# Two graph layers on one core: a new instruction order for the first two groups, the set-up's weight sums on three engines, and one transpose moved behind one addition

## The chip, the cores and the metric

The kernel runs on one core of a Trainium2 chip. The metric is the device time of one execution in microseconds; the median of three runs of the kernel before is 2593.3 us (2591.22 to 2593.96).

## What is computed

The input x holds 128 graphs of 128 nodes with 512 features. Two layers follow each other, each on a layer norm with ReLU, each added to its input. In the reference's terms, cut to what matters:

```python
h = maximum(layernorm(x), 0)
q, k, v = h @ Wq0.T, h @ Wk0.T, h @ Wv0.T
rel = adj.T * (q @ k.T)
x = x + (rel / norm(rel, axis=2)) @ v                       # layer 0
h = maximum(layernorm(x), 0)
q, k, v = h @ Wq1 + bq, h @ Wk1 + bk, h @ Wv1 + bv          # 8 heads of 64
x = x + softmax(q @ k.T / 8 + mask(adj == 0)) @ v           # layer 1
```

All of it is float32.

## The kernel before, in words

The 128 graphs are worked in 32 groups of four. Five products of a 512x512 matrix with a group's turned h (512 features x 512 nodes) carry most of the arithmetic: g and v of layer 0 (g is h times Wq0.T Wk0, a matrix made once in `weights0`), and Q, K, V of layer 1. Each is a `Product`, done with seven half-sized products P1 to P7 instead of eight (the method of Strassen and Winograd). For this each weight matrix is kept as seven 256-column parts: three plain quarters and four sums T1, T2, T3, T4N, made once by `sums` (lines 91 to 96); the fourth plain quarter, `w12`, is needed only for the sums. The data side has four sums too, s0 to s3 (`sumA`, `sumB`). P1 to P7 accumulate in three PSUM banks x, y and z: P6, P7 and P4 are added on top of what P1 left in bank x, P3 on top of P5 in bank z. ScalarE or VectorE copies the bank out after P1, P5 and P6 (`keep`), and VectorE adds a kept part to the bank and writes a quarter of the result after P2, P3 and P7 (`add`, line 232). So **P7 must wait until the copy after P6 has read bank x, and P4 until P7's addition has read it.**

h has to be turned, features on partitions. In the first group TensorE does it against an identity (`turn_pe`). In all others it is done through memory: `hn` (ScalarE) writes the normalised rows, sends them to DRAM, `rd` (SyncE's queue) fetches them back in blocks, and `T` (VectorE, line 303) turns 32x32 blocks of what came back. `T0` makes the first half of h (two graphs), `T1` the second. P1 and P2 read the first half, P5, P6, P3 need sums over both halves, P7 needs another sum, P4 the second half.

Other steps that the prediction names: `stat` (VectorE, means and variances) and `inv` (GpSimd, four small operations that make scale and shift) come ahead of `hn`. `R` makes rel for four graphs, `mask_rel`, `square`, `N` and `norms` mask it and make the norms (the last step on GpSimd), `O` multiplies rel with v and `xO` adds to x. `S`, `mk`, `ex`, `wr`, `wt` are scores, mask with row maximum, exponentials with the way to DRAM, the fetch, and the turning of the softmax weights; `A` multiplies them with v; `oc`, `rdo`, `ot` turn and add the output. GpSimd adds to x and stores.

The order of work is written out by hand: the schedule is manual on all five engines, so every engine executes its instructions in the order in which they are issued, and `run` issues one step after another from a list of names. In a step's name, p is layer 1 of two groups ago, l layer 1 of the last group, m layer 0 of this group, n layer 1 of this group, f layer 0 of the next. There is one list, `ORDER` (lines 517 to 526), used for all 32 groups, and `LAST` for the tail. In the first group p and l do not exist and their steps are skipped, and so are m's steps of turning. The set-up ahead of it is `weights0`, `turn_pe` twice, `weights_v0`, and `weights1`, which scales Wq1 and bq and makes twelve sums, all on GpSimd.

Buffers that matter: four PSUM banks for the products (`ps_mm`), two for rel, O and A (`ps_o`), one pair for the scores (`ps_s`). Each half of h and each s has a single buffer per layer.

Of the kernel before, what the change touches and what calls it, by code (L numbers as in the profile page):

```python
# [9 lines left out]
F32 = mybir.dt.float32  # L10
AF = mybir.ActivationFunctionType
ALU = mybir.AluOpType
AX = mybir.AxisListType

P = 128
# [6 lines left out]
def kernel(  # L22
# [15 lines left out]
    nc = tc.nc  # L38
    B, N, D = x.shape
    assert N == P and B % G == 0  # L40
    KD = D // P
    H, HD = 8, 64
# [20 lines left out]
    ps_o = ctx.enter_context(tc.tile_pool(name="ps_o", bufs=2, space=PSUM))  # L63
# [4 lines left out]
    def load(g: int, b: int, queue):  # L68
        xb = xpool.tile([P, D], F32, tag="xb", name=f"xb_{g}_{b}")
        queue.dma_start(xb, x[g * G + b])  # L70
        x_tiles[g, b] = xb

    for b in range(G):
# [13 lines left out]
    wc = {  # L87
        n: const.tile([P, 7, 2, HF], F32, tag=f"wc_{n}", name=f"wc_{n}") for n in ("a", "v0", "q", "k", "v1")
    }

    def sums(n: str, w12, eng):
        c = wc[n]
        eng.tensor_tensor(c[:, T1], w12, c[:, W11], ALU.subtract)
        eng.tensor_tensor(c[:, T2], c[:, W22], c[:, T1], ALU.subtract)
        eng.tensor_tensor(c[:, T3], c[:, W22], w12, ALU.subtract)
        eng.tensor_tensor(c[:, T4N], c[:, W21], c[:, T2], ALU.subtract)
# [11 lines left out]
    bq_sb = const.tile([P, NH], F32, tag="bq", name="bq_sb")  # L108
    bk_sb = const.tile([P, NH], F32, tag="bk", name="bk_sb")
    bv_sb = const.tile([P, H * HD], F32, tag="bv", name="bv_sb")  # L110
    w12 = {}

    def place(n: str, m: int, ps, w12, copy):

        copy(wc[n][:, W11 if m < 2 else W21, m % 2, :], ps[:, 0:HF])
        copy(w12[:, m, :] if m < 2 else wc[n][:, W22, m % 2, :], ps[:, HF:D])

    def weights0():

        a12 = rpool.tile([P, 2, HF], F32, tag="r", name="a12")  # L120
        pa = [ps_mm.tile([P, D], F32, tag="mm", name=f"pa_{m}") for m in range(KD)]
        for k in range(KD):
            for m in range(KD):
                nc.tensor.matmul(
                    pa[m], lhsT=raw["q"][:, k, ts(m, P)], rhs=raw["k"][:, k, :],
                    start=(k == 0), stop=(k == KD - 1),
                )
        for m in range(KD):
            place("a", m, pa[m], a12, nc.vector.tensor_copy)
        sums("a", a12, nc.vector)  # L130

    def weights_v0():
        v12 = rpool.tile([P, 2, HF], F32, tag="r", name="v12")
        for m in range(KD):
            pt = ps_mm.tile([P, KD, P], F32, tag="mm", name=f"pwv_{m}")
            for k in range(KD):
                nc.tensor.transpose(pt[:, k, :], raw["v"][:, k, ts(m, P)], ident)
            place("v0", m, pt.rearrange("p k e -> p (k e)"), v12, nc.scalar.copy)
        sums("v0", v12, nc.gpsimd)
        nc.vector.tensor_scalar(mask, adj_sb, 0.0, NEG, ALU.is_equal, ALU.mult)  # L140

    def load1():
        for name, w in (("q", wq1), ("k", wk1), ("v1", wv1)):
            wr = w.rearrange("(k p) d -> p k d", p=P)
            nc.gpsimd.dma_start(
                wc[name][:, W11 : W21 + 1].rearrange("p h k d -> p (h k) d"), wr[:, :, 0:HF]
            )
            nc.gpsimd.dma_start(wc[name][:, W22], wr[:, 2:4, HF:D])
            w12[name] = wpool.tile([P, 2, HF], F32, tag="wT", name=f"w12_{name}")
            nc.gpsimd.dma_start(w12[name], wr[:, 0:2, HF:D])  # L150
        nc.gpsimd.dma_start(bq_sb, bq1.rearrange("(e p) -> p e", p=P))
        nc.gpsimd.dma_start(bk_sb, bk1.rearrange("(e p) -> p e", p=P))
        nc.gpsimd.dma_start(bv_sb, bv1.partition_broadcast(P))

    def weights1():

        SC = HD**-0.5
        nc.gpsimd.tensor_scalar(wc["q"][:, 0:3], wc["q"][:, 0:3], SC, None, ALU.mult)
        nc.gpsimd.tensor_scalar(w12["q"], w12["q"], SC, None, ALU.mult)
        nc.gpsimd.tensor_scalar(bq_sb, bq_sb, SC, None, ALU.mult)  # L160
        for n in ("q", "k", "v1"):
            sums(n, w12[n], nc.gpsimd)


    EN = mybir.EngineType
# [89 lines left out]
    class Layer:  # L255
# [49 lines left out]
                self.u.pop(i).rearrange("p t (k q) -> p t k q", q=BK),  # L305
            )

        def turn_pe(self, i):

            half = self.half_tile(i)  # L310
            hn = npool.tile([P, 2, KD, P], F32, tag="e", name=f"hn_{i}")
            for r in range(2):
                b = 2 * i + r
                nc.scalar.activation(
                    hn[:, r].rearrange("p k q -> p (k q)"), x_tiles[self.g, b], AF.Relu,
                    bias=self.shift[:, b : b + 1], scale=self.rstd[:, b : b + 1],
                )
                pt = ps_o.tile([P, KD, P], F32, tag="po", name=f"pt_{b}")
                for k in range(KD):
                    nc.tensor.transpose(pt[:, k, :], hn[:, r, k, :], ident)  # L320
                nc.scalar.copy(half[:, :, ts(r, P)], pt)
# [29 lines left out]
    class Layer0(Layer):  # L351
        n = 0
# [54 lines left out]
    class Layer1(Layer):  # L407
        n = 1
# [105 lines left out]

    ORDER = """
        l.Q.P1 p.rdo0 l.sumA l.Q.P2 m.hn0 l.sumB l.K.P1 m.rd0 m.hn1 l.K.P2 m.rd1 p.wt3 l.Q.P5
        p.ot0 l.Q.P6 l.Q.P3 p.A1 p.oc1 p.rdo1 m.T0 l.Q.P7 l.K.P5 m.T1 l.K.P6 l.Q.P4 f.load0 f.load1
# [2 lines left out]
        l.ex1 l.wr1 l.wt0 m.R m.mask_rel m.square f.stat2 f.stat3 f.inv1 m.V.P6 m.V.P3 m.N m.norms l.S2 l.mk2  # L522
        m.V.P7 l.ex2 l.wr2 l.wt1 m.O0 m.xO0 m.O1 m.xO1 n.stat0 n.stat1 n.inv0 m.V.P4 n.hn0 n.rd0 l.start_v l.V.P1
        m.O2 m.xO2 m.O3 m.xO3 n.stat2 n.stat3 n.inv1 l.S3 l.mk3 l.V.P2 l.V.P5 n.hn1 l.V.P6 l.wt2 n.rd1 l.ex3
        l.wr3 l.V.P3 n.T0 l.V.P7 l.A0 l.oc0 l.V.P4 n.T1 n.start
    """.split()
    LAST = """
        l.Q.P1 p.rdo0 l.sumA l.Q.P2 l.sumB l.K.P1 l.K.P2 p.wt3 l.Q.P5 p.ot0 l.Q.P6 l.Q.P3 p.A1 p.oc1
# [2 lines left out]
        l.V.P4 l.ex3 l.wr3 l.wt1 l.A0 l.oc0 l.rdo0 l.wt2 l.wt3 l.A1 l.oc1 l.rdo1 l.ot0 l.ot1  # L531
    """.split()

    def run(order, m=None, **who):
        who["m"] = m
        for step in order:
            name, *path = step.split(".")
            at = who.get(name)
            if at is None or (name == "m" and m.g == 0 and path[0][:-1] in ("hn", "rd", "T")):
                continue  # L540
            if len(path) == 2:
                getattr(getattr(at, path[0]), path[1])()
            elif path[0][-1].isdigit():
                getattr(at, path[0][:-1])(int(path[0][-1]))
            else:
                getattr(at, path[0])()

    with tc.manual_schedule(engines={EN.PE, EN.SP, EN.Pool, EN.DVE, EN.Activation}):
        p, l, m = None, None, Layer0(0)
        for b in range(G):  # L550
            m.stat(b)
        m.inv(0)
        m.inv(1)
        for b in range(G):
            load(1, b, nc.gpsimd)
        load1()
        weights0()
        m.turn_pe(0)
        m.turn_pe(1)
        weights_v0()  # L560
        weights1()
        for g in range(NG):
            n = Layer1(g)
            f = Layer0(g + 1) if g + 1 < NG else None
            run(ORDER, p=p, l=l, m=m, n=n, f=f)
            p, l, m = l, n, f
        run(LAST, p=p, l=l)

# [29 lines left out]
```

## Time and profile before

| what | value |
|---|---|
| median of three runs | 2593.3 us |
| the profiled execution | 2595.17 us |
| span of its instructions | 2593.4 us, mean granted TensorE clock 0.99 |
| TensorE busy | 2513.8 us (97%) |
| VectorE, ScalarE, GpSimd busy | 1701.2 us (66%), 1020.6 us (39%), 549.7 us (21%) |
| first matmul of layer 1's Q in the first group | at 80.05 us |
| the same in the second group | at 159.82 us |
| from there to the last group's | 30 groups, 77.57 to 79.63 us each |

One execution was traced. A time is the distance from the first instruction. TensorE appears twice, as PE (matmul) and PEld (weight load). Each of the seven products issues four float32 matmuls, and the trace holds two records for each of these, so that a product is a row of "x8". "DVE" is VectorE, "ACT" ScalarE, "POOL" GpSimd, "SP" SyncE. A row of the timeline gives start, duration, engine, line, operation, what is written and read, and in brackets how long the engine had been idle and what ended that.

### The profile page before, as it was taken

Reading aid. Unit: us, or ns where it says so; the run is one execution under the profiler, and the core shown is the slowest. Engines: PE = TensorE matmul, PEld = TensorE weight load, DVE = VectorE, ACT = ScalarE, POOL = GpSimd, SP = SyncE. Lnnn points to the kernel's source line nnn. Section 1 sums busy time; section 2 is a strip of 40 time slices with the busy share of each in tenths; the row PEclk is TensorE's granted clock in tenths of the full one; section 3 lists DMA queues with packets and bytes.
Section 4 is the critical chain, followed back from the end, with each engine's and each line's share of the span. In section 5 each row is a group of like instructions: output and inputs, shape, how many; then the busy total and the mean of one; then the engine's idle time right before and its main releaser. Section 6 shows DMA issues by size and latency. Waiting matters only on the chain.

```text
span 2593.4 us, 40797 instructions
## 1 busy us (share of the span) xinstructions
PE 2513.8 (97%) x14656; PEld 2135.5 (82%) x14656; DVE 1701.2 (66%) x2477; ACT 1020.6 (39%) x3245; POOL 549.7 (21%) x961
## 2 busy tenths in 40 slices
PE   8799999999999999999999999999999999999995
PEld 6688888888888888888888888888888888888884
DVE  3466766667666667666667666667666666666664
ACT  2334443344333444334444334444334344434442
POOL 6012122212122112122112221121222121222111
PEclk9899999999999999999999999999999999999997
DMA  3255444555445555445554445454445554445443
GB/s 135 98 163 194 140 147 154 175 167 183 148 137 167 171 171 180 139 145 167 167 179 158 147 143 175 160 194 149 146 145 178 163 190 144 145 156 172 162 139 130
DMA packets 374379, 409.90 MB, mean 158 GB/s; under 512 B 29920, under 2 KB 290144, under 8 KB 374176
## 3 DMA queue, kind: packets, MB, share of 16 engines
q1 hardware_dynamic: 281168, 167.92, 22.8%
q10 hardware_dynamic: 71792, 169.89, 17.6%
q0 software_dynamic: 21216, 69.49, 7.7%
q8 instruction: 115, 1.88, 0.3%
q14 instruction: 88, 0.72, 0.1%
HBM read 206.90 MB, written 200.28 MB: 157 GB/s over the span
## 4 chain that ended last, share of the span: by engine, by line
PE 80%; DVE 7%; DMA 7%; POOL 2%; issue 2%; SPq 1%; ACT 1%; DVEq 0%; POOLq 0%; ACTq 0%
PE pv_x L208 12%; PE pq_x L208 9%; PE pk_x L208 8%; PE pg_x L208 8%; PE pv_z L208 5%; PE pg_z L208 4%; PE pk_z L208 4%; PE pr L367 4%; PE pss L430 4%; PE pq_z L208 4%; DMA u_h<-d_h 4%; PE po L476 3%; PE po L399 3%; PE pv_y L208 3%; PE pq_y L208 2%; PE pk_y L208 2%
## 5 line engine op out<-in xcount | busy, mean ns | idle before, releaser
L448 ACT ACTIVATE e<-pss,nmax 128x128 f32<-128x128 f32 x1024 | 359.7, 379 | 203.5 <-DVE nmax L441 185.5
L511 POOL TENSOR_TENSOR xb<-xb,o 128x512 f32<-128x512 f32 x128 | 163.2, 1275 | 1193.4 <-DVE o L504 1191.7
L208 PE MATMUL pv_x<-wc_v,h 128*128 128x256 f32 x1280 | 301.9, 383 | 21.7 <-DVE v L232 21.3
L208 PEld LDWEIGHTS pv_x<-wc_v,h 128*128 128x128 f32 x1280 | 241.4, 191 | 74.4 <-DVE v L232 39.0
L291 ACT ACTIVATE hn<-xb,shift,rstd 128x512 f32<-128x512 f32 x252 | 190.9, 807 | 155.7 <-POOL shift L283 150.8
L208 PE MATMUL pv_z<-wc_v,s 128*128 128x256 f32 x1024 | 245.2, 382 | 0.0
L303 DVE STREAM_TRANSPOSE h<-u_h 128x1024 f32<-128x1024 f32 x126 | 156.4, 1241 | 104.3 <-DMA u_h<-d_h 103.8
L448 ACT ACTIVATION_READ_ACCUMULATOR e<-pss,nmax 128x1 f32 x1024 | 224.2, 219 | 0.0
L439 DVE TENSOR_TENSOR pss<-pss,mask 128x1024 f32<-128x1024 f32 x128 | 157.2, 1228 | 99.5 <-PE pss L430 99.3
L208 PEld LDWEIGHTS pv_z<-wc_v,s 128*128 128x128 f32 x1024 | 192.1, 190 | 28.7 <-DVE pv_r L225 0.3
L208 PE MATMUL pq_x<-h,wc_q 128*128 128x256 f32 x768 | 186.4, 386 | 14.6 <-issue 14.6
L208 PE MATMUL pv_x<-wc_v,s 128*128 128x256 f32 x768 | 184.9, 384 | 0.0
L208 PE MATMUL pk_x<-h,wc_k 128*128 128x256 f32 x768 | 181.5, 379 | 0.0
L208 PEld LDWEIGHTS pq_x<-h,wc_q 128*128 128x128 f32 x768 | 144.6, 191 | 39.0 <-issue 15.4
L273 DVE BATCH_NORM_STATS2 st<-xb 128x6 f32<-128x512 f32 x256 | 172.1, 672 | 5.2 <-DMA xb<-in_x_dram 5.2
L280 POOL TENSOR_SCALAR rstd<-mv 128x2 f32<-128x2 f32 x128 | 28.6, 224 | 648.8 <-DVE mv L274 648.6
L430 PEld LDWEIGHTS pss<-kT,qT 64*128 64x128 f32 x2048 | 124.7, 188 | 48.7 <-PE po L399 23.5
L208 PEld LDWEIGHTS pk_x<-h,wc_k 128*128 128x128 f32 x768 | 146.0, 190 | 19.8
L441 DVE TENSOR_REDUCE nmax<-pss 128x8 f32<-128x1024 f32 x128 | 156.7, 1224 | 4.4
L463 DVE STREAM_TRANSPOSE wT<-u_w 128x1024 f32<-128x1024 f32 x128 | 152.8, 1194 | 8.0 <-DMA u_w<-d_w 8.0
L208 PEld LDWEIGHTS pv_x<-wc_v,s 128*128 128x128 f32 x768 | 140.9, 190 | 20.3
L430 PE MATMUL pss<-kT,qT 64*128 64x128 f32 x2048 | 149.5, 285 | 2.5 <-ACT e L448 2.3
(134 smaller groups left out, 4438.4 us busy)
## 6 DMA issues: line engine op xcount, KB each, us to landing
d_w<-e ACTq DMA_DIRECT2D x128, 512.0 KB, 2.6
u_w<-d_w SPq DMA_DIRECT2D x512, 128.0 KB, 2.9
d_h<-hn ACTq DMA_DIRECT2D x126, 512.0 KB, 3.4
u_h<-d_h SPq DMA_DIRECT2D x504, 128.0 KB, 3.3
d_o<-oT ACTq DMA_DIRECT2D x64, 512.0 KB, 3.9
u_o<-d_o SPq DMA_DIRECT2D x256, 128.0 KB, 3.3
out_dram<-xb POOLq DMA_DIRECT2D x128, 256.0 KB, 2.8
xb<-in_x_dram POOLq DMA_DIRECT2D x124, 256.0 KB, 3.3
```

The lines of the kernel that those rows point to most:

```text
L208: nc.tensor.matmul(ps[:, m, :], lhsT=lhsT, rhs=rhs, start=first and m == 0 and k == 0, stop=k == 1, skip_group_check=True,)
L273: nc.vector.bn_stats(st, x_tiles[g, b])
L291: nc.scalar.activation(hn[:, r], x_tiles[g, b].rearrange("p (k j q) -> p j k q", j=TB, q=BK), AF.Relu, bias=self.shift[:, b : b + 1], scal ...
L303: nc.vector.transpose(half.rearrange("p k (t i) -> p t k i", i=BK), self.u.pop(i).rearrange("p t (k q) -> p t k q", q=BK),)
L367: nc.tensor.matmul(pr[:, b, :], lhsT=self.turned(k, b), rhs=self.gT[:, k, ts(b, P)], start=(k == 0), stop=(k == KD - 1),)
L399: nc.tensor.matmul(po, lhsT=self.rel[:, b, :], rhs=self.v[:, b, :], start=True, stop=True)
L430: nc.tensor.matmul(pss[:, r, k, :], lhsT=self.qT[rows, k, ts(b, P)], rhs=self.kT[rows, k, ts(b, P)], start=True, stop=True,)
L439: nc.vector.tensor_tensor(sc, sc, mask[:, None, :].to_broadcast([P, H, P]), ALU.add)
L441: nc.vector.tensor_reduce(self.nmax[b], sc, AX.X, ALU.max, negate=True)
L448: nc.scalar.activation(e[:, :, i, :], sc[:, i, :].rearrange("p (j q) -> p j q", q=BK), AF.Exp, bias=nmax[:, i : i + 1], accum_out=self.tot ...
L463: nc.vector.transpose(self.wT[b].rearrange("p h (t i) -> p t h i", i=BK), self.uw.pop(b).rearrange("p t (h q) -> p t h q", q=BK),)
L511: nc.gpsimd.tensor_tensor(xb, xb, o.rearrange("p k t q -> p (k t q)"), ALU.add)
```

## The change

Four things are done, all of them moves:

1. **Set-up.** The normalised rows of the first group's h are made by their own step `hn_pe`, ahead of `weights0`. The eight TensorE transposes of the first half are issued between the third and the fourth quarter of `weights0`'s matmuls, those of the second half behind the last quarter.
2. **Layer 1's weights.** The scaling of Wq1 and bq goes from GpSimd to ScalarE, the four sums of q and the four of k go to VectorE, those of v1 stay on GpSimd. They are no longer issued in one piece but as steps `w.scale`, `w.sumq`, `w.sumv`, `w.sumk` within the first group's list.
3. **First two groups.** They get lists of their own, `FIRST` and `SECOND`. In FIRST the second group's h is made and turned during the first group's layer 0, and the second group's seven g products (`f.G`) stand right behind the first group's O2 and O3, ahead of its layer 1. SECOND is ORDER without these steps and without the steps of p.
4. **All other groups.** In ORDER the step `n.T0` goes from before `l.V.P7` to behind it.

```diff
-    def weights0():
+    def weights0(between):
...
+            if k == KD - 2:
+                between()
...
-    def weights1():
-
-        SC = HD**-0.5
-        nc.gpsimd.tensor_scalar(wc["q"][:, 0:3], wc["q"][:, 0:3], SC, None, ALU.mult)
-        nc.gpsimd.tensor_scalar(w12["q"], w12["q"], SC, None, ALU.mult)
-        nc.gpsimd.tensor_scalar(bq_sb, bq_sb, SC, None, ALU.mult)
-        for n in ("q", "k", "v1"):
-            sums(n, w12[n], nc.gpsimd)
+    class Weights1:
+        def scale(self):
+
+            SC = HD**-0.5
+            nc.scalar.mul(wc["q"][:, 0:3], wc["q"][:, 0:3], SC)
+            nc.scalar.mul(w12["q"], w12["q"], SC)
+            nc.scalar.mul(bq_sb, bq_sb, SC)
+
+        def sumq(self):
+            sums("q", w12["q"], nc.vector)
+
+        def sumk(self):
+            sums("k", w12["k"], nc.vector)
+
+        def sumv(self):
+            sums("v1", w12["v1"], nc.gpsimd)
...
+    FIRST = """
+        m.sumA m.sumB m.start m.G.P1 w.scale m.G.P2 f.stat0 f.stat1 f.inv0 m.G.P5 f.hn0 f.rd0 m.G.P6 w.sumq
+        m.G.P3 f.stat2 f.stat3 f.inv1 m.V.P1 f.hn1 f.rd1 w.sumv m.G.P7 m.V.P2 w.sumk m.G.P4 m.V.P5
+        m.R m.mask_rel m.square f.T0 m.V.P6 m.V.P3 m.N m.norms m.V.P7 m.O0 m.xO0 m.O1 m.xO1 n.stat0 n.stat1
+        n.inv0 n.hn0 n.rd0 m.V.P4 f.T1 m.O2 m.O3 f.sumA f.start f.G.P1 m.xO2 m.xO3 n.stat2 n.stat3 n.inv1
+        n.hn1 n.rd1 f.G.P2 f.sumB f.G.P5 f.G.P6 f.G.P3 n.T0 f.G.P7 f.G.P4 n.T1 n.start
+    """.split()
+    SECOND = """
+        l.Q.P1 l.sumA l.Q.P2 l.sumB l.K.P1 l.K.P2 l.Q.P5 l.Q.P6 f.load0 f.load1 l.Q.P3 l.K.P5 l.K.P6 l.Q.P7
+        l.K.P3 l.K.P7 l.S0 l.mk0 f.load2 f.load3 l.Q.P4 l.K.P4 l.ex0 l.wr0 m.V.P1 f.stat0 f.stat1 f.inv0
+        m.V.P2 l.S1 l.mk1 m.V.P5
+        l.ex1 l.wr1 l.wt0 m.R m.mask_rel m.square f.stat2 f.stat3 f.inv1 m.V.P6 m.V.P3 m.N m.norms l.S2 l.mk2
...
     ORDER = """
...
-        l.wr3 l.V.P3 n.T0 l.V.P7 l.A0 l.oc0 l.V.P4 n.T1 n.start
+        l.wr3 l.V.P3 l.V.P7 n.T0 l.A0 l.oc0 l.V.P4 n.T1 n.start
...
         load1()
-        weights0()
-        m.turn_pe(0)
+        m.hn_pe(0)
+        m.hn_pe(1)
+        weights0(lambda: m.turn_pe(0))
         m.turn_pe(1)
         weights_v0()
-        weights1()
...
-            run(ORDER, p=p, l=l, m=m, n=n, f=f)
+            run((FIRST, SECOND, ORDER)[min(g, 2)], p=p, l=l, m=m, n=n, f=f, w=Weights1())
```

SECOND ends with the same steps as the new ORDER, `l.V.P7 n.T0` included.

More of the change, by code (lines that the diff above doesn't have):

```diff
@@ L306, in T, with hn_pe @@
             )
-        def turn_pe(self, i):
-            half = self.half_tile(i)
+        def hn_pe(self, i):
             hn = npool.tile([P, 2, KD, P], F32, tag="e", name=f"hn_{i}")
@@ L317, in turn_pe @@
                 )
-                pt = ps_o.tile([P, KD, P], F32, tag="po", name=f"pt_{b}")
+            self.d[i] = hn
+        def turn_pe(self, i):
+            half, hn = self.half_tile(i), self.d.pop(i)
+            for r in range(2):
+                pt = ps_o.tile([P, KD, P], F32, tag="po", name=f"pt_{2 * i + r}")
                 for k in range(KD):
@@ L512, in ot @@
                 nc.gpsimd.dma_start(out[g * G + b], xb)
+    FIRST = """
[10 more added lines that the diff above has]
+        l.ex1 l.wr1 l.wt0 m.R m.mask_rel m.square f.stat2 f.stat3 f.inv1 m.V.P6 m.V.P3 m.N m.norms l.S2 l.mk2
+        m.V.P7 l.ex2 l.wr2 l.wt1 m.O0 m.xO0 m.O1 m.xO1 n.stat0 n.stat1 n.inv0 m.V.P4 n.hn0 n.rd0 l.start_v l.V.P1
+        m.O2 m.xO2 m.O3 m.xO3 n.stat2 n.stat3 n.inv1 l.S3 l.mk3 l.V.P2 l.V.P5 n.hn1 l.V.P6 l.wt2 n.rd1 l.ex3
+        l.wr3 l.V.P3 l.V.P7 n.T0 l.A0 l.oc0 l.V.P4 n.T1 n.start
+    """.split()
     ORDER = """
@@ L524 @@
         m.O2 m.xO2 m.O3 m.xO3 n.stat2 n.stat3 n.inv1 l.S3 l.mk3 l.V.P2 l.V.P5 n.hn1 l.V.P6 l.wt2 n.rd1 l.ex3
-        l.wr3 l.V.P3 n.T0 l.V.P7 l.A0 l.oc0 l.V.P4 n.T1 n.start
+        l.wr3 l.V.P3 l.V.P7 n.T0 l.A0 l.oc0 l.V.P4 n.T1 n.start
     """.split()
@@ L532, with run @@
     """.split()
-    def run(order, m=None, **who):
-        who["m"] = m
+    def run(order, **who):
         for step in order:
@@ L538, in run @@
             at = who.get(name)
-            if at is None or (name == "m" and m.g == 0 and path[0][:-1] in ("hn", "rd", "T")):
+            if at is None:
                 continue
```

## The prediction

> **What bounds the kernel now.** I read the page first, then who waited for whom on TensorE, then the timeline of one boundary between two groups and of the first 82 us, then the windows.
>
> The page has TensorE busy for 97% of the span and on 80% of the chain that ended last, so only TensorE's idle time and its slow clock can be won. Its waits are few:
>
> ```profile
> PE pv_x L208 <- DVE v L232: 21.3, 22, 2.0
> PE pq_x L208 <- issue: 14.6, 1, 14.6
> PE pa L124 <- DMA raw_k<-in_L_gnn_Wk_dram: 5.8, 1, 5.8
> PE pt L320 <- ACT hn L314: 4.2, 3, 1.4
> PE po L399 <- DVE xb L405: 1.1, 1, 1.1
> ```
>
> (waiting instruction, releaser: us in total, times, longest.) All five but the load are touched. The first is the only one that recurs. Group 16's end shows it, VectorE first, then TensorE:
>
> ```profile
> 1405.79 0.65 DVE L232 TENSOR_TENSOR v<-pv_z,pv_r 128x512 f32<-128x512 f32 x1
> 1409.38 1.25 DVE L303 STREAM_TRANSPOSE h<-u_h 128x1024 f32<-128x1024 f32 x1 [2.94 <-DMA u_h<-d_h]
> 1410.55 0.65 DVE L232 TENSOR_TENSOR v<-pv_x,pv_r 128x512 f32<-128x512 f32 x1
> ```
>
> ```profile
> 1407.30 1.97 PE L476 MATMUL po<-wT,v 128*64 128x128 f32 x32
> 1411.26 1.99 PE L208 MATMUL pv_x<-wc_v,h 128*128 128x256 f32 x8 [1.99 <-DVE v L232]
> 1413.09 1.89 PE L208 MATMUL pq_x<-h,wc_q 128*128 128x256 f32 x8
> ```
>
> V.P7 ended about 1407.4. Its addition (1410.55) stood behind T0, which waited 2.94 us for a transfer; so V.P4 on the same bank waited 1.99 us behind A0. The 22 waits are this one with other landings.
>
> The start, by windows (TensorE's busy time is the first number after the length, the granted clock stands after POOL):
>
> ```profile
> 24.50:27.80 3.30, 0.90 (x7) 0.42 (x5) 1.22 (x3) 2.27 (x4) 0.00 (x0) 1.00 0.71 206
> 27.90:31.20 3.30, 3.02 (x14) 3.03 (x15) 1.22 (x2) 1.62 (x5) 0.00 (x0) 0.50 0.00 0
> 31.30:34.70 3.40, 3.40 (x20) 3.08 (x19) 2.45 (x3) 2.16 (x7) 2.86 (x2) 1.00 0.00 0
> 68.90:80.00 11.10, 0.00 (x0) 0.00 (x0) 1.25 (x1) 1.52 (x2) 2.27 (x5) 0.50 0.72 236
> 80.10:85.80 5.70, 5.70 (x14) 4.55 (x15) 2.63 (x3) 1.96 (x4) 0.00 (x0) 0.50 0.02 5
> ```
>
> Here TensorE has nothing from 65.5 to 80.05, while layer 1's h goes through memory (d_h is issued at 68.93, T0 starts at 78.70: 9.8 us). After that it runs 5.8 us at half clock, 2.9 us lost.
>
> **Part 4, T0 behind P7's addition.** The addition then starts at P7's end and takes 0.65 us, under A0's 1.90 us: V.P4 follows A0 without a wait. What is queued behind is T0, and its reader Q.P1, which comes 1.90 + 1.73 = 3.6 us after A0's start. By the landings of the fetches, T0's data came between 0.2 us before A0's start and 1.96 us after it, so T0 ends at 3.3 us at the latest: covered, with 0.3 to spare (cover ends at a landing of 2.3 us). T1 comes next: its data landed 4.5 to 6.8 us after A0's start; with T1 (1.24) and two sums (0.7 each) it is ready at 9.5 at most, and its reader Q.P5 starts at 3.6 + 4 x 1.73 = 10.5. In the four groups whose T0 was early the distance to the next group was 77.57 us each, with nothing late: that is the state that all reach. The distance from the second group's Q (159.82) to the last's (2509.37) is 2349.55 us; 30 x 77.57 is 2327.1. The excess is 22.4 us; the gaps on PE alone sum to 20.4. I take **21.5**, and 17 to 22.4 for a few late landings. The 31st gap, 1.29 us at 158.0, is counted with the start.
>
> **Part 1, turning h amid the weights' product.** Before, the last matmul pass of `weights0` ends at 22.26, the turning (four times 0.45 with three waits of 1.39) at 29.1, then 16 transposes at half clock, and G.P1 starts at 31.91. The normalised rows are ready in time: ACT is free from 9.56, four times 0.81, with the second pair's scale at 11.39, so all by 13.0, well ahead of 18.8, the end of the third quarter (22.26 less 8 passes of 0.43). After: 18.8 + 0.9 + 3.44 + 0.9, and 16 transposes at 0.11, a quarter of 0.45 (1.8): G.P1 at 25.9, **6.0 earlier**. [...] The row above, 27.9 to 31.2, holds transposes alone, and the clock came back to 1.00 behind it. [...]
>
> **Part 2, the sums on three engines.** Before, GpSimd worked on sums and scaling from 31.77 to 58.3, and the norms waited behind it until 62.6: that cost the 1.1 us ahead of O2. It goes. ScalarE's scaling is not in the trace; a copy of 256 takes 0.37 and of 512 0.58, so 1536 take about 1.5, with the other two 2.3: it stands ahead of no copy that is due (G.P5's follows 0.5 us later), so 0, at most 0.5. What is new is that VectorE and GpSimd work on two-input sums at the same time. The only place that shows this:
>
> ```profile
> 31.40 0.69 DVE L345 TENSOR_TENSOR s<-h,s 128x512 f32<-128x512 f32 x1
> 32.01 1.78 DVE L346 TENSOR_TENSOR s<-h,h 128x512 f32<-128x512 f32 x1
> ```
>
> ```profile
> 31.77 1.48 POOL L93 TENSOR_TENSOR wc_v<-v,wc_v 128x512 f32<-128x512 f32 x1 [7.75 <-ACT v L116]
> 33.32 1.60 POOL L94 TENSOR_TENSOR wc_v<-wc_v 128x512 f32<-128x512 f32 x1
> ```
>
> VectorE's sum lasted until 0.5 us after GpSimd's end, and GpSimd's next one was longer by 0.3: they took turns. Now G comes early, so that all four of s0 to s3 (from 26.7) meet GpSimd's four sums of v0 (from 26.4): four pairs of 1.15 + 0.55, s2 at about 32.9 instead of 29.5. The queue behind: G.P2's addition (33.6), two `stat` (1.6, as from 64.05 to 65.66 before: 35.2), `inv0` (1.6, as from 65.75 on: 36.9), and on ScalarE `f.hn0` (1.5, and 0.4 to issue) stands **ahead of the copy after G.P6**: 38.9 to 39.5. G.P7 would start at 36.4 and waits 3.1 us. Without the turn-taking the same count gives 0.6; with every pair lost 3.3. I take **3.1**, by the nearest row. Sumk against sumv end by 50.3, at the end of R (50.0): nothing.
>
> Clock: [...] But in 24.5 to 27.8 TensorE was busy for 0.90 of 3.30 us and the clock halved behind it. [...] by the row up to 1.7, [...]: **0.9**.
>
> **Part 3, FIRST.** The 14.6 us of idle time and the 2.9 us of slow clock go. New waits:
> - ScalarE's order in FIRST has n.hn0 ahead of V.P4's copy, and O2 reads what that copy writes. From O0's start (58.83 before): O1's xO ends at 61.45 (norms no longer late), two stats 1.61, inv0 1.7, hn 1.52, DMA issue 0.4, copy 0.6: O2 at 67.4. V.P4 ends at 62.4. **Idle 5.05 us**, certain by the order. It is longer than the idle share that halved the clock above; [...]. Loss 1.4 to 3.0: **2.1**.
> - f.G then covers the way through memory: from O2, two O and seven G take 1.7 + 12.1 us. n.T0's data is there 9.8 us after its hn, before G.P3 ends. But FIRST has n.T0 *ahead of* G.P7's addition: 1.25 us of T0 before it, P4 waits **0.95**. T1's data comes 3.5 us or more before Q.P5.
>
> In SECOND the G products are gone between S0 and A0. From Q.P1 on: S0 at 20.8, nmax at 24.5, kT's copy until 26.35, exponentials 2.85: S1 (28.9) waits 0.4. The softmax weights are fetched 8.3 us after (d_w issued at 29.25): `wt0` at 37.6 to 38.8 holds mask_rel, square and so N back to 40.3, instead of 39.2. Together **1.5**, from 0.5 to 3.5. Later fetches have the distances of ORDER.
>
> Sum of the start: gains 6.0 + 1.1 + 14.6 + 2.9 + 1.3 = 25.9; costs 3.1 + 0.9 + 5.05 + 2.1 + 0.95 + 1.5 = 13.6; net 12.3. With part 4 it is 33.8. The profiled execution took 2595.17, 1.9 above the median and 1.8 above its own span; the difference is taken from the median: 2593.3 - 33.8 = **2559.5**.
>
> **Rivals.**
> 1. *The start is smooth*: the engines do not take turns, G.P7 waits 0.6, little clock is lost: costs 0.6 + 5.05 + 1.4 + 0.95 + 0.5 = 8.5, net 17.4, with 22.4 in the groups: **2553.5**. For it: 0.69 in most rows of L341 to L346. Against: none of those had GpSimd at work. 15%.
> 2. *The set-up gains nothing*: G.P7's wait, O2's wait and two clock drops eat all of it, and only part 4 remains: **2572**. For it: ScalarE's order. Against: over 14 us of costs at their upper ends are needed. 10%.
> 3. *The wait moves*: Q.P1 waits for T0 where V.P4 did. It needs landings over 2.3 us after A0, 31 rows have none. **2581**. 6%.
> 4. *Slower*: T1. TensorE reaches Q.P5 up to 2 us earlier, T1's data does not. Q.P2's addition stands behind T1 and the sums on VectorE and frees the bank for Q.P5, so that from a landing of 7.2 us after A0 on each group waits. The latest of 31 was 6.8. For a loss it would take 8.4 on average; at 8.7, 31 x 1.5 = 46 us: **2606**. 3%.
>
> **How the numbers follow.** About 64% stands on 2559.5, its own range 2554 to 2567. The 80% range takes in the first rival's edge and half the second: 2552 to 2569. What a measurement can tell from no change is 0.2%, 5.2 us. Faster by more than that 95%, within it 2% (what the cases leave over), slower by more 3%.
>
> **What the changed profile would show.** V.P4's wait for v's addition is gone from TensorE's waits, and groups are 77.6 us apart; if not, part 4 is wrong. G.P1 at about 26. G.P7 waits about 3 us for a copy by ScalarE, and s0 to s3 last over 1 us each; 0.69 would mean rival 1. O2 waits 5 us, with half clock after it. Q.P1 of the first group at about 81, the second group's at about 147. T0's gap ahead of Q.P1, or Q.P5's wait, would show rivals 3 and 4.

## The result and the profile after

The changed kernel takes 2561.65 us (median of four runs, 2561.03 to 2562.56) against 2593.19 for the kernel before: a ratio of 0.988 with a 95% interval of 0.9863 to 0.9897, 31.5 us less, where 2559.5 was forecast. Its profiled execution took 2561.42 us with a span of 2559.6.

TensorE's waits in the changed kernel (line 219 are the products' matmuls, 415 is O, 492 is A, 227 a copy by ScalarE, 243 an addition by VectorE, 479 the turning of the softmax weights):

```profile
PE po L492 <- DVE wT L479: 7.0, 2, 5.5
PE pa L124 <- DMA raw_k<-in_L_gnn_Wk_dram: 6.1, 1, 6.1
PE po L415 <- ACT v L227: 5.4, 1, 5.4
PE pg_x L219 <- ACT pg_r L227: 5.0, 1, 5.0
...
PE pg_x L219 <- DVE gT L243: 0.9, 1, 0.9
```

The recurring wait (21.3 us, 22 times) and the 14.6 us ahead of the first Q are gone. A's waits are the tail's. Three waits of 5.4, 5.0 and 0.9 us are new, all in FIRST. Ahead of O2, the longest, ScalarE's copy of what V.P4 made stands behind `n.hn0`, which itself waited for GpSimd's shift, though V.P4 had ended at 63.26:

```profile
66.02 1.52 ACT L302 ACTIVATE hn<-xb,shift,rstd 128x512 f32<-128x512 f32 x2 [9.93 <-POOL shift L294]
...
68.03 0.58 ACT L227 COPY v<-pv_x 128x512 f32<-128x512 f32 x1 [0.49 <-ACT hn L302]
```

The boundary at the end of group 16, as shown of before, first VectorE (314 is T0), then TensorE:

```profile
1386.86 0.69 DVE L243 TENSOR_TENSOR v<-pv_x,pv_r 128x512 f32<-128x512 f32 x1 [0.97 <-PE pv_x L219]
1387.47 1.24 DVE L314 STREAM_TRANSPOSE h<-u_h 128x1024 f32<-128x1024 f32 x1
```

```profile
1386.76 1.97 PE L492 MATMUL po<-wT,v 128*64 128x128 f32 x32
1388.65 1.99 PE L219 MATMUL pv_x<-wc_v,h 128*128 128x256 f32 x8
1390.48 1.89 PE L219 MATMUL pq_x<-h,wc_q 128*128 128x256 f32 x8
```

P7's addition starts 0.1 us after A0, T0 follows, and V.P4 stands directly behind A0 without a wait. T0's end (1388.71) leaves Q.P1 1.8 us.

The new idle stretches, by windows (TensorE's busy time after the length; the granted clock after POOL):

```profile
24.00:25.80 1.80, 1.80 (x19) 1.80 (x18) 1.77 (x4) 1.80 (x6) 0.00 (x0) 1.00 0.90 221
36.20:41.20 5.00, 0.10 (x1) 0.00 (x0) 2.01 (x4) 2.05 (x4) 2.17 (x4) 1.00 0.02 7
41.40:44.80 3.40, 3.40 (x9) 2.66 (x10) 2.12 (x5) 0.34 (x1) 0.97 (x3) 0.52 0.48 169
65.60:72.20 6.60, 3.53 (x4) 1.51 (x5) 1.77 (x3) 2.10 (x3) 0.38 (x1) 0.50 0.30 108
72.40:76.00 3.60, 3.60 (x19) 3.17 (x18) 2.30 (x6) 0.58 (x1) 0.93 (x2) 1.00 0.27 79
```

After each of the two stretches, 5.00 and 5.41 us without work, the clock is at half, and 3.4 and 3.5 us of work run at half speed.

Where the time came from, in spans: up to the second group's Q 149.28 instead of 159.82 (10.5 us), from there to the last group's Q 2327.21 instead of 2349.55 (22.3 us, every distance 77.57 or 77.63), the tail 83.1 instead of 84.0 (0.9 us).

### The profile page after: what moved, and what is told of

Its sections match the earlier page's. It is cut to its first block, busy times and chain, and to the rows that moved or that the text cites. A ratio compares the mean times of both kernels' runs of the same rounds, so it can differ in the third digit from the quotient of the medians.

```text
span 2559.6 us, 40828 instructions
## 1 busy us (share of the span) xinstructions
PE 2509.3 (98%) x14656; PEld 2131.7 (83%) x14656; DVE 1714.1 (67%) x2485; ACT 1022.0 (40%) x3248; POOL 538.1 (21%) x950
## 3 DMA queue, kind: packets, MB, share of 16 engines
q1 hardware_dynamic: 281168, 167.92, 23.3%
## 4 chain that ended last, share of the span: by engine, by line
PE 96%; DVE 1%; DMA 1%; ACT 1%; issue 0%; POOL 0%; SPq 0%; ACTq 0%; POOLq 0%; DVEq 0%
PE pv_x L219 17%; PE pq_x L219 9%; PE pv_z L219 9%; PE pk_x L219 9%; PE pg_x L219 9%; PE pss L446 5%; PE po L492 5%; PE pr L383 4%; PE pv_y L219 4%; PE pg_z L219 4%; PE po L415 4%; PE pk_z L219 4%; PE pq_z L219 4%; PE pq_y L219 2%; PE pk_y L219 2%; PE pg_y L219 2%
```

## The experiments

The theory is that the waits are separate: each has its own queue, and what it costs comes back when that queue's order is mended. The rivals were that only one part gains, that layer 1's way through memory sets the start's time whatever the order, or that an engine named in a wait only shows it. The kernels of one batch ran on one chip, beside the kernel before (median 2592.39 in the first batch and in the third, 2591.85 in the second). Two things differ from trace to trace that none of these edits is about: the clock first came to 1.00 between 9.35 and 12.43 us, which is worth up to 1.5 us (half of the difference, as TensorE is busy then: in the changed kernel the matmuls of line 124 follow each other after 0.85 us ahead of that change, at 10.84, and after 0.43 behind it), and the tail, the time from the last group's Q on, lasted from 83.1 to 84.4 us.

**T0 behind P7's addition, alone**, in the kernel before:

```diff
-        l.wr3 l.V.P3 n.T0 l.V.P7 l.A0 l.oc0 l.V.P4 n.T1 n.start
+        l.wr3 l.V.P3 l.V.P7 n.T0 l.A0 l.oc0 l.V.P4 n.T1 n.start
```

> The kernel before with only the step n.T0 moved behind l.V.P7. Theory (each of the 31 boundaries loses its wait of V.P4 and nothing else is late): the 22.4 us of the 30 distances between groups and the 1.3 us of the first, so 2593.2 - 23.7 = 2569.5 us, all distances 77.57 to 77.65, the start up to 155 us as before. Rival (the regular distances need the new start, or the wait moves to Q.P1 or Q.P5): 2580 or more, with those waits among TensorE's.

Measured: 2571.12 us, ratio 0.9916 (0.9901 to 0.993). The first Q of the second group is at 157.92, and from the second group's to the last's it is 2328.5 us, 1.3 more than in the changed kernel, most of it in one place:

```profile
PE pq_x L208 <- DVE h L303: 0.8, 1, 0.8
```

There, one time in 31, T0's data landed 3.3 us after A0's start, past the 2.3 us that the prediction gave as the end of the cover, and Q.P1 waited: its third rival, once. Even so, this one move of a step carries about two thirds of the whole gain, and it does not need the new start. Its four runs lie within 2570.4 and 2571.87, where nine of the kernel before on the same chip go from 2588.58 to 2595.99: this fits a spread that came mostly from when T0's data landed (only one execution of each was traced).

**Everything else, without it**: the changed kernel with `n.T0 l.V.P7` in both lists.

> The changed kernel with n.T0 put back ahead of l.V.P7 in ORDER and SECOND. Theory (the parts add up): 2561.7 + 22.4 to 24 = 2584 to 2586 us, about 9 below the kernel before, and the first Q at 85.5 as in the changed kernel. Rival (the start's gain is the larger part): 2575 or less.

Measured: 2585.09, ratio 0.997 (0.9957 to 0.9982). V.P4's wait for v's addition is back, 18.7 us in 18 times, and the first Q is at its new place. Against the kernel before on that chip the two parts alone give 21.3 and 7.3 us, 28.6 together, against 31.5 for the change: they add up within the spread of those nine runs, 7.4 us.

**G.P6's copy ahead of f.hn0** in FIRST:

```diff
-        m.sumA m.sumB m.start m.G.P1 w.scale m.G.P2 f.stat0 f.stat1 f.inv0 m.G.P5 f.hn0 f.rd0 m.G.P6 w.sumq
+        m.sumA m.sumB m.start m.G.P1 w.scale m.G.P2 f.stat0 f.stat1 f.inv0 m.G.P5 m.G.P6 f.hn0 f.rd0 w.sumq
```

> The changed kernel with f.hn0 and f.rd0 behind m.G.P6 in FIRST, so that ScalarE copies bank x before it waits for the second group's scale. Theory: G.P7 starts at 36.1 instead of 41.3 and the clock does not halve at 41.6; next late is G.P7's addition, behind sumq, G.P3's addition and two stats on VectorE, for which G.P4 waits about 1.6 us; O2 keeps its wait of 5.4. Net 5.3 us: 2556.3. Rival (G.P7 waits for VectorE's or the DMA's part, and ScalarE's order only shows it): within 1 us of 2561.7.

Measured: 2557.38, ratio 0.9861 (0.9847 to 0.9876). G.P7 follows V.P1 at once, the clock stays at 1.00 there, the second group's Q comes 5.4 us earlier (143.92), and the next late thing is the one named:

```profile
37.24 1.89 PE L219 MATMUL pv_y<-wc_v,h 128*128 128x256 f32 x8
40.46 1.99 PE L219 MATMUL pg_x<-h,wc_a 128*128 128x256 f32 x8 [1.33 <-DVE gT L243]
```

It was ScalarE's order: the copy had nothing to wait for but its place.

**V.P4's copy ahead of n.hn0** in FIRST:

```diff
-        n.inv0 n.hn0 n.rd0 m.V.P4 f.T1 m.O2 m.O3 f.sumA f.start f.G.P1 m.xO2 m.xO3 n.stat2 n.stat3 n.inv1
+        n.inv0 m.V.P4 n.hn0 n.rd0 f.T1 m.O2 m.O3 f.sumA f.start f.G.P1 m.xO2 m.xO3 n.stat2 n.stat3 n.inv1
```

> The changed kernel with n.hn0 and n.rd0 behind m.V.P4 in FIRST. Theory: O2's wait falls from 5.4 to about 0.8 us and the half clock from 65.5 to 72.3 is gone (1.8 us), so G.P1 of the second group starts 6.5 us earlier; but n.T0, whose data comes 9.8 us after its issue at 67.6, stands ahead of G.P7's addition on VectorE, and G.P4 waits 3.2 us for it instead of 0.9. Net 4.5 us: 2557.2. Rival A (all of the 7 us come through): 2554.8. Rival B (layer 1's way through memory set the time, O2's wait was covered by it): 2561.

Measured: 2557.82, ratio 0.9865 (0.985 to 0.9879). O2's wait is 0.7 instead of 5.4, with no slow clock after it (O2 and O3 took 1.98 us instead of 3.77). The sum is as expected, its parts are not: G.P4 waits 0.85 as before, not 3.2, and G.P3 waits 1.54 for a copy that now stands behind n.hn1 on ScalarE. The same kind of fault had come up one step later. In the trace the second group's Q came 5.8 us earlier (143.50), 0.7 of this by the first return of the clock (9.35 against 10.84), and the tail was 1.3 us longer; that the time meets the forecast is in part luck.

**That one mended too, and n.T0 taken behind G.P4**:

```diff
-        n.hn1 n.rd1 f.G.P2 f.sumB f.G.P5 f.G.P6 f.G.P3 n.T0 f.G.P7 f.G.P4 n.T1 n.start
+        f.G.P2 f.sumB f.G.P5 n.hn1 n.rd1 f.G.P6 f.G.P3 f.G.P7 f.G.P4 n.T0 n.T1 n.start
```

> The kernel with V.P4's copy first, and in addition n.hn1 and n.rd1 behind f.G.P5, and n.T0 behind f.G.P4. Theory after the first four runs: G.P3's wait of 1.5 us for a copy behind n.hn1 goes, but G.P4's wait of 0.85 stays, as it is the time of G.P7's own addition with nothing between the two on TensorE, and not T0's: 2557.8 - 1.7 = 2556.1. Rival (T0 ahead of the addition makes that wait, as the prediction has it): it goes as well, 2555.2.

Measured: 2557.26, no gain on the last one that could be told apart. G.P3's wait is gone, but:

```profile
77.27 1.99 PE L219 MATMUL pg_x<-h,wc_a 128*128 128x256 f32 x8 [0.78 <-DVE gT L243]
...
88.35 2.66 PE L219 MATMUL pq_z<-s,wc_q 128*128 128x256 f32 x8 [2.18 <-DVE qT L243]
```

G.P4 still waits 0.78, with T0 nowhere near: this is P7's own addition, since in FIRST nothing stands between P7 and P4 on TensorE. And Q.P5 now waits for Q.P2's addition, which stands on VectorE behind T1 and two sums, at half clock for 3.4 us afterwards: the mechanism of the prediction's fourth rival, not in the groups but in the start.

**The sums of v0 behind f.inv0** on GpSimd:

```diff
-        sums("v0", v12, nc.gpsimd)
+        w12["v0"] = v12
...
+        def early(self):
+            sums("v0", w12["v0"], nc.gpsimd)
...
-        m.sumA m.sumB m.start m.G.P1 w.scale m.G.P2 f.stat0 f.stat1 f.inv0 m.G.P5 f.hn0 f.rd0 m.G.P6 w.sumq
+        m.sumA m.sumB m.start m.G.P1 w.scale m.G.P2 f.stat0 f.stat1 f.inv0 w.early m.G.P5 f.hn0 f.rd0 m.G.P6 w.sumq
```

> The changed kernel with GpSimd's four sums of v0 issued behind f.inv0 in FIRST instead of ahead of it, so that GpSimd is idle while VectorE makes s0 to s3. Theory (the two take turns): these four last 0.69 us each instead of 1.65 to 1.75, s2 is ready at 29.6 instead of 33.5, inv0 starts 3 us earlier, G.P7 waits about 1.4 us instead of 5.0, and the clock stays at full speed: 5.5 us less, 2556.2. Rival (the sums are slow for another reason, such as their operands): within 1 us of 2561.7.

Measured: 2558.11, ratio 0.9866 (0.985 to 0.9883). With GpSimd idle, s0 to s3 last 0.69 us each. The first pair of rows shows two of them in this run, the second pair the same two in the changed kernel, where the first of the four took 0.68 us and the others 1.64 to 1.75:

```profile
28.07 0.69 DVE L361 TENSOR_TENSOR s<-s,h 128x512 f32<-128x512 f32 x1
28.79 0.69 DVE L364 TENSOR_TENSOR s<-h,s 128x512 f32<-128x512 f32 x1
```

```profile
28.51 1.65 DVE L358 TENSOR_TENSOR s<-s,h 128x512 f32<-128x512 f32 x1
30.20 1.64 DVE L361 TENSOR_TENSOR s<-h,s 128x512 f32<-128x512 f32 x1
```

G.P7's wait fell from 5.0 to 1.1 us and the clock held (G.P7 took 1.99 us instead of 3.56), so the turns between the engines are the cause. The gain is 2 us under the expected, and the clock accounts for it. It first came to 1.00 at 11.93 us instead of 10.84 (0.5 us), and after O2's wait, 5.41 us as before, TensorE worked for 6.2 us at half clock instead of 3.5 (1.3 us). In the changed kernel the clock was at half from 65.46 to 72.28, and 3.2 us of this passed before O2 started (68.67). Here it was at 0.50 from 63.8 to 70.0, and O2 had started at 63.72.

**All transposes behind weights0's last matmul**, the rows still made ahead of it:

```diff
-            if k == KD - 2:
-                between()
...
-        weights0(lambda: m.turn_pe(0))
+        weights0(None)
+        m.turn_pe(0)
```

> The changed kernel with all transposes behind weights0's last matmul; the normalised rows stay ahead of it. Theory (the gain at G.P1 comes from making the rows early, not from turning amid the product): G.P1 within 0.6 us of 25.8. The copies of weights0's result start 0.9 us earlier on VectorE, so G.P7's wait falls by up to 1.5: 2560 to 2562. Rival (turning amid the product is what gains): G.P1 at 27.5 or later, 2563.5 or more.

Measured: 2560.5 us, not to be told from the changed kernel. G.P1 starts at 27.13 instead of 25.78, but 0.8 of this is the clock's: it came back at 12.4 us instead of 10.8, half of the difference being lost work. What remains is 0.5. So it is `hn_pe` ahead of the product that gained most of the 6 us, and turning amid the product is worth half a microsecond there; G.P7's wait is shorter by 2.3 (2.7 instead of 5.0): TensorE comes to it 1.35 us later, and `inv0` ends 1.0 earlier (37.64 instead of 38.6), since here VectorE's mask was not held by GpSimd's sums (0.22 us instead of 1.32). No slow clock came behind the transposes: from 23.3 to 27.1 us TensorE did nothing else, with one gap of 0.24, and the clock stayed at 1.00 (the last sixteen took 1.91 us, 0.11 each, where the kernel before has 0.21 at half clock, and G.P1 behind them took 1.89).

**All of it together**: both copies first, the sums of v0 later, and in the second group's g an order with one product between any two on the same bank:

```diff
-        n.hn1 n.rd1 f.G.P2 f.sumB f.G.P5 f.G.P6 f.G.P3 n.T0 f.G.P7 f.G.P4 n.T1 n.start
+        f.G.P2 f.sumB f.G.P6 n.hn1 n.rd1 f.G.P5 f.G.P7 f.G.P3 n.T0 f.G.P4 n.T1 n.start
```

> All of it together: f.hn0 behind m.G.P6, the sums of v0 behind f.inv0, V.P4's copy ahead of n.hn0, n.hn1 behind f.G.P6, and the second group's g products in the order P1 P2 P6 P5 P7 P3 P4, which leaves one product between any two on the same bank. Theory (the waits are separate, so what each costs adds up): TensorE's waits of 5.0, 5.4, 1.5 and 0.9 us and both stretches of half clock are gone, Q of the second group at about 136 instead of 149.3: 2548.5. Rival (layer 1's way through memory, 9.5 us from its issue, takes their place ahead of Q.P1): 2552 or more.

Measured: 2550.76, ratio 0.984 (0.9825 to 0.9854), and, on another chip, 2549.88. That is 2.3 us above the expected: the second group's Q is at 137.60 instead of 136. All four waits, G.P4's included, and both slow stretches are gone, but for 0.7 us ahead of O2. What came up is Q.P5's wait for Q.P2's addition, 2.1 us in this trace and 1.1 in that of the repetition. For that:

```diff
-        f.G.P2 f.sumB f.G.P6 n.hn1 n.rd1 f.G.P5 f.G.P7 f.G.P3 n.T0 f.G.P4 n.T1 n.start
+        f.G.P2 f.sumB f.G.P6 n.hn1 n.rd1 f.G.P5 f.G.P7 f.G.P3 n.T0 f.G.P4 n.start
...
-        l.Q.P1 l.sumA l.Q.P2 l.sumB l.K.P1 l.K.P2 l.Q.P5 l.Q.P6 f.load0 f.load1 l.Q.P3 l.K.P5 l.K.P6 l.Q.P7
+        l.Q.P1 l.Q.P2 l.T1 l.sumA l.sumB l.K.P1 l.K.P2 l.Q.P5 l.Q.P6 f.load0 f.load1 l.Q.P3 l.K.P5 l.K.P6 l.Q.P7
```

> The version with all of it together, with n.T1 and the sums behind it taken behind Q.P2's addition on VectorE (T1 goes from FIRST's end into SECOND). Theory (Q.P5's new wait of 2.1 us is for the bank that Q.P2's addition frees at 80.4, behind T1 and two sums, as the prediction's fourth rival describes it; its own sum s0 is there at 79.1): the wait falls to 0.8, Q of the second group at 136.3 instead of 137.6, 1.3 us less than that version on the same chip. Rival (the wait is for T1's data itself): no change.

> The version with all of it together once more, for the comparison on one chip: within 2 us of 2550.8.

Measured: 2547.87 us, ratio 0.9829 (0.9816 to 0.9843), 2.0 us under the version it was made from on the same chip; Q of the second group is at 135.64 against 137.40. Of these 1.8 us in the two traces, 1.1 is the first return of the clock (10.14 against 12.27); the way from the first group's Q to the second's, which the move is about, is 0.7 shorter (64.65 against 65.32). The move's own worth thus stays between 0.7 and 2.0 us. The wait is now for T1's data by way of the sum:

```profile
76.63 1.25 DVE L317 STREAM_TRANSPOSE h<-u_h 128x1024 f32<-128x1024 f32 x1 [1.16 <-DMA u_h<-d_h]
77.91 0.69 DVE L360 TENSOR_TENSOR s<-h 128x512 f32<-128x512 f32 x1
```

```profile
78.75 1.97 PE L222 MATMUL pq_z<-s,wc_q 128*128 128x256 f32 x8 [0.61 <-DVE s L360]
```

This is the fastest version, 13.8 us under the changed kernel's median and 44.5 under that of the kernel before on its chip.

## Why the prediction was right, and where its sizes were off

- **T0 behind the addition**: 21.5 was the forecast, 22.3 came, the whole excess over 77.57. T0's data landed between 0.13 us before A0's start and 1.59 after it; T0 ended at least 0.7 us ahead of Q.P1, so the cover held in all 31 of this trace. The run of that part alone shows the gain, and also that the cover can fail: once there, for 0.8 us.
- **Turning h amid the product**: G.P1 at 25.78, forecast 25.9. Nothing was lost to the clock behind the transposes, neither here (G.P1 took 1.89 us) nor in the run with all of them behind the product (1.89 as well). The step named the wrong half of the edit as its title: the rows made ahead are what gains.
- **The sums on three engines**: the turn-taking was right (the run with GpSimd idle shows it: 0.69 us each, where three of the four took 1.64 to 1.75 here). s2 was ready at 33.5; the prediction wrote 32.9, but its own estimate, four pairs of 1.70 us from 26.7 on, adds up to 33.5. That this sum fits is in part luck: three of the sums were slowed, not four, and in place of s0 (0.68 us) the mask ahead of it was (1.32 instead of 0.22). The term that was mis-sized is inv0, taken as 1.6 us from a row in which VectorE did other work. It took 2.8 us. In the changed kernel it ran beside sumq, and each of three small operations took 0.35 to 0.44 us more than in the undisturbed inv1 (rows of GpSimd; 0.57 against 0.22, 1.15 against 0.71, 0.64 against 0.23):

```profile
35.82 0.57 POOL L291 TENSOR_SCALAR rstd<-mv 128x2 f32<-128x2 f32 x1 [2.85 <-DVE mv L285]
36.48 1.15 POOL L292 TENSOR_TENSOR rstd<-rstd,mhalf 128x2 f32<-128x2 f32 x1
37.69 0.64 POOL L293 TENSOR_SCALAR shift<-mv 128x2 f32<-128x2 f32 x1
...
43.67 0.22 POOL L291 TENSOR_SCALAR rstd<-mv 128x2 f32<-128x2 f32 x1 [5.07 <-DVE mv L285]
43.98 0.71 POOL L292 TENSOR_TENSOR rstd<-rstd,mhalf 128x2 f32<-128x2 f32 x1
```

  No run took sumq away from inv0, so that cause rests on these rows. With that and s2's 0.6, G.P7 waited 5.0 instead of 3.1 us, and the clock drop, put at 0.9 as a half chance, came in full: 1.7.
- **O2**: 5.41 us against 5.05, and 1.8 lost to the clock against 2.1; removed when the copy goes first.
- **G.P4's 0.95**: 0.85, right in size for the wrong reason. T0 ended at 83.08, about when P7 did, and the addition started at 83.01; the wait is the addition's own, and taking T0 away left it (0.78).
- **SECOND**: 1.5 was set, 0.27 came. S1 waited for the exponentials as said; the softmax weights were fetched 7.3 us after their issue instead of 8.3, so that `square` ended 0.2 us ahead of N.
- **The start's sum**: 25.9 of gains less 5.0 + 1.7 + 5.4 + 1.8 + 0.85 + 0.3 = 15.05 is 10.9; 10.5 was measured, 12.3 forecast. One sign was off: the first group's Q.P1 came at 85.55, not at about 81. The prediction's own terms, added up from G.P1 on, give about 82; the larger wait of G.P7 with its clock drop makes most of the rest. The tail's 0.9 us, in code that was not changed, was not forecast; it lies within what the tail differs by from trace to trace. In spans the change gave 33.8 us, exactly the forecast sum. That is luck: 1.8 us too little in the start, 0.8 and 0.9 too much in the groups and the tail.
- **The time itself** came out 2.15 us above the forecast. The profiled execution of before lay 1.9 us above its median, that of after 0.2 below its own, and I took the full difference of spans from the median. If the runs of before differ mainly in how long V.P4 waits, which one trace cannot show, the profiled one had more to lose than the median run; a gain read from a varying wait should have been scaled to the median.

## What to carry to other kernels

On an engine that works in order, ask of every short instruction that frees a buffer what stands ahead of it: an addition behind a transfer, or a copy behind an activation that waits for statistics, makes another engine idle though its own data is long there. When such a step is moved ahead, follow the queue once more, because the next one of the same kind is often right behind it (here three in a row), and give two matmul groups on one accumulator something in between (here G.P4 directly behind G.P7 waited 0.78 us, with a product between them not at all). Spreading work over two engines that then work side by side on two-input operations is not free: here a pair took 1.7 us, where the two alone take 0.69 and 1.27. Cost each such pair at nearly the sum of the two, and watch small operations beside them too.

## What the hardware showed that I had not expected

- The clock was at half behind a TensorE gap of 2.69 us (the run with all transposes behind the product, 6.8 us at 0.50) and behind one of 2.18 us (the run with n.T0 behind G.P4, 3.4 us at 0.50). It stayed at 1.00 behind one of 2.08 us (all of it together, 80.6 to 84.0) and behind the 1.99 us of the kernel before (at 1411.26).
- The length of the slow stretches, as the traces of the kernel before and of the changed kernel have it ahead of the tail: 3.41 us (before, from 27.87, and changed, from 41.56), 6.83 (changed, from 65.46) and 17.07 (before, from 68.83). In the 3.41 us just ahead of them TensorE was busy for 0.28, 0.07, 0.36 and 0.02 of the time, in their last 3.41 us for 0.91, 1.00, 1.00 and 1.00. A low share just ahead is not enough by itself: the 3.41 us that end with the gap of 2.08 us were busy for 0.39, and the clock stayed at 1.00. What decides was not shown.
- A VectorE instruction with one tensor input was held as well: the mask's 128x128 operation took 1.32 us beside GpSimd's sums in the changed kernel and 0.22 with GpSimd idle (the run with the sums of v0 later).
